# Tokens sorted by expert inside their tile, and moved to the experts' pages in runs of 64 rows

## The chip, the cores and the metric

One Trainium2 chip, one core of it. The metric is the device time of one launch in microseconds (us). The time before is the median of 14 runs, 3545.61 us (3536.86 to 3567.67).

The engines are called PE (matrix products; PEld is its load of weights), DVE (vector), ACT (scalar), POOL (GpSimd) and SP (sync). Each takes its instructions in program order from a queue of its own, and the transfers (DMAs) that an engine issues stand in that queue between its other instructions.

## The reference

A graph layer, and behind it a layer of experts, on x with 12500 rows (tokens) of 256 numbers and 212500 edges that are sorted by dst:

```
msgs = layernorm(x)[src] * edge_weight[:, None]
x = x + segment_sum(msgs, dst) @ W.T + b

h = layernorm(x)
probs = softmax(h @ gate_w + gate_b)               # 8 experts
idx, prb = argmax(probs), the probability there
pos = how many earlier tokens chose the same expert
kept = pos < C                                     # C = 1954
y = relu(h @ w1[idx] + b1[idx]) @ w2[idx] + b2[idx]   # 256 -> 1024 -> 256
x = x + nan_to_num(y * (prb * kept))
```

All numbers are float32. The tokens of an expert have places 0, 1, 2, ... in the order of their row, and those at C and above get nothing from the expert.

## The kernel before

**Units.** An *edge tile* is 128 edges; there are 1661 (`KT`). A *node tile* is 128 tokens; there are 98, each the target of some 17 edge tiles. Node tiles go in *chunks*: eleven of 8, then 5, 4 and 1. A *page* is 128 rows of one expert in the tensor `buf` in DRAM, 16 pages an expert and two spare. A row of `buf` has 260 numbers (`RW`): the token after the graph layer, its mean and inverse deviation, its probability, and its row number. A row of a page with number `FILL` (1048576) is empty; an output scatter drops rows out of bounds.

**Phases.** `table()` writes the normalized x to DRAM (`feat`); the first 112 edge tiles are gathered meanwhile from x itself. Then the loop `while alive or pages or b or outs` (L822) does the rest. One turn of it issues, in this order:

1. `gather(s)` (L582, POOL): an indirect transfer of 128 rows of 1 KB from `feat` to one of 32 buffers `m`.
2. one item of `pool_q`, if there is one: a `put` (L341, POOL), an indirect transfer that scatters the rows of one node tile (`rt`) to their pages by the index `to`. If there is none, one step of `outs`, the end of a page's work: DVE makes `z` and `tok` (L522), and `send` (L525, POOL) scatters the page's rows to the output.
3. one-hots (L590, DVE, four at a time, 8 ahead of the products) and `product(done)` (L599, PE), the edge product of the tile gathered 16 turns (`LEAD`) earlier; 15 products sum up to one group (`ws`, L602, ACT).
4. one step of `nodes()`, one of `fill()` or `check()` at the beginning, and one of `experts()`.

`nodes()` goes over the chunks. For each node tile it loads x (`xt`, L623, three tiles ahead, issued by ACT), places the groups' sums by products with shifted one-hots (L635), copies (L639), multiplies by W (L644) and adds (L647). At the end of the chunk `route` stores the chunk's rows to the output (`store_rows`, L170, issued by ACT), normalizes, gates (L274, L279), and finds each token's place: `pp` counts the tokens of each expert before a token in its tile (`pp[:, 0]`) and in the whole tile (`pp[:, 1]`), `run` counts over the tiles (L321 and the line after it). The puts of the chunk then wait in `pool_q`. `listing` (L370 is in it, on DVE) finds which pages have become full. When `pool_q` is empty, these pages are queued:

```
SLOTS = [(2, n) for n in (0, 3, 4, 4, 4, 4, 4, 4, 4, 2)] + [(1, n) for n in (10, 4, 3)]
```

(pages at a time, and how many times, after each chunk but the last: chunk 0 none, chunk 1 three pairs, and so on). After the last chunk come the 8 partly filled pages, whose places `last` gives.

`experts()` takes queued pages. `load` (SP) reads the page's row and expert into registers (L432, L435), then issues the page's transfer (`pg`, L439) and `weights` its biases (L446, L448) and weights (L450, L452), whose addresses are in those registers. `LOADED - 3` = 17 turns later `fresh` (L459, DVE) normalizes the page, at 20 turns `turn` (L468) transposes it, then `products` (L483, L487, L494) is spread over turns, 3.0 turns a step for a pair (`PACE`). `fill()` writes empty rows to all of `buf` at the start of the loop, 13 transfers of SP.

**Order.** Everything runs under `tc.manual_schedule()`: each engine does its instructions in the order in which the program issues them. Waits come from the data (and from buffers that come free); `declare_no_dep` takes back those between puts and between puts and page loads.

After the loop, `rest()` runs only if more full pages are left, and a second path (`tc.If(some > 0)`) only if `n_bad`, a count of edges that lie out of the expected windows, isn't 0.

Of the kernel before, what the change touches and what calls it, by code (L numbers as in the profile page):

```python
# [18 lines left out]
P = 128  # L19
# [26 lines left out]
FILL = float(1 << 20)  # L46


SLOTS = [(2, n) for n in (0, 3, 4, 4, 4, 4, 4, 4, 4, 2)] + [(1, n) for n in (10, 4, 3)]
# [9 lines left out]
LOADED = 20  # L59
PACE = {1: 2.3, 2: 3.0}  # L60


# [32 lines left out]
def gnn_moe_kernel(ctx: ExitStack, tc: tile.TileContext, x, src, dst, ew, wT, gb, gate_w, gate_b,  # L95
# [53 lines left out]
    nc.vector.tensor_scalar(need, even, float(P), float(P), op0=ALU.mult, op1=ALU.add)  # L149
    n_bad = consts.tile([1, 1], I32, name="n_bad")  # L150

    gb_sb = consts.tile([P, D], F32, name="gb_sb")
# [4 lines left out]
    keep = ctx.enter_context(tc.tile_pool(name="keep", bufs=1))  # L157
    run = keep.tile([P, E], F32, name="run")
    posted = keep.tile([P, 1], F32, name="posted")
    place_of = keep.tile([P, 1], F32, name="place_of")  # L160
# [58 lines left out]
    class Ffn:  # L219
        def __init__(self, p3, p4, ps_m, ps_t, ps_h, ps_y):  # L220
            self.p3, self.p4 = p3, p4
            self.ps_m, self.ps_t, self.ps_h, self.ps_y = ps_m, ps_t, ps_h, ps_y
            self.puts, self.sends, self.loads = [], [], []
            self.paired = False
# [6 lines left out]
            nc.vector.memset(taken, 0.0)  # L231

        def fill(self):
# [11 lines left out]

        def route(self, rt, ln, t0, nt, rows):
            p3 = self.p3
            yield
            r = yield from ln_scale(p3, ln, nt, rows)
            o = store_rows(out, rt[:, :, :D], t0, nt, rows, nc.scalar)  # L250
            for i in self.sends:
# [99 lines left out]

            self.put = [(put, j) for j in range(nt)]


# [57 lines left out]
        def last(self):  # L412
            p3 = self.p3
            c8 = p3.tile([P, E], F32, name="c8")
            nc.vector.tensor_mul(c8, run, mine)
            c = p3.tile([P, 1], F32, name="c1")
            nc.vector.tensor_reduce(c, c8, axis=AX.X, op=ALU.add)
            nc.vector.tensor_scalar(c, c, float(C), page0, op0=ALU.min, op1=ALU.subtract)
            some = p3.tile([P, 1], F32, name="some")
            nc.vector.tensor_scalar(some, c, 1.0, None, op0=ALU.is_ge)  # L420
            nc.vector.scalar_tensor_tensor(some, c, float(P), some, op0=ALU.is_lt, op1=ALU.mult)
            nc.vector.tensor_scalar(c8, mine, some, None, op0=ALU.mult)
            pi = self.psum("pi")
            nc.tensor.matmul(pi[0:1, :E], page_of[:, 0:1], c8, start=True, stop=True)
            lp = p3.tile([1, E], I32, name="lp", bufs=1)
            nc.vector.tensor_scalar(lp, pi[0:1, :E], float(NP_ * P), None, op0=ALU.add)
            return lp

        def load(self, of, li, i, e=None):
            p4 = self.p4  # L430
            at = li[0:1, 0, i:i + 1] if e is None else li[0:1, e:e + 1]
            row = nc.values_load(at, engines=[mybir.EngineType.SP], min_val=0, max_val=NP_ * P,  # L432
                                 skip_runtime_bounds_check_because="a page, or the empty one")
# [4 lines left out]
            pg = p4.tile([P, 2, RW], F32, name="pg", bufs=4)  # L438
            self.loads.append(nc.sync.dma_start(  # L439
                pg[:, :of, :], buf[ds(row, of * P), :].rearrange("(a p) d -> p a d", p=P)))  # L440
# [118 lines left out]
    with tc.tile_pool(name="edges", bufs=1) as edges:  # L559
# [8 lines left out]
        with tc.tile_pool(name="p2", bufs=32) as p2, tc.tile_pool(name="p2h", bufs=12) as p2h, \  # L568
# [8 lines left out]
            sums, ms, hs = {}, {}, {}  # L577
            pool_q, pages = [], []

# [25 lines left out]
            def nodes():  # L605
# [10 lines left out]
                for c, (t0, nt, rows) in enumerate(CHUNKS):  # L616
                    rt = p3.tile([P, CH, RW], F32, name="rt")
                    ln = ln_new(p3)
                    for t in range(t0, t0 + nt):
                        for i in range(len(xs), min(t + 3, NT)):  # L620
                            x_ = p3.tile([P, D], F32, name="xt", bufs=4)
                            r = min(P, N - i * P)
                            nc.scalar.dma_start(x_[:r, :], x[i * P:i * P + r, :])  # L623
                            xs.append(x_)
# [24 lines left out]
                        ln_stats(ln, x1, t - t0, rows)  # L649
                    yield from ffn.route(rt, ln, t0, nt, rows)  # L650
                    pool_q.extend(ffn.put)
                    last = c == len(CHUNKS) - 1
                    if last or SLOTS[c][1]:
# [4 lines left out]
                        while pool_q:  # L658
                            yield
# [62 lines left out]
            def check():  # L722
# [17 lines left out]
                nc.tensor.matmul(pc, ones[:, 0:1], cnt, start=True, stop=True)  # L740
                nc.vector.tensor_scalar(n_bad, pc, -1.0, float(P * KT), op0=ALU.mult, op1=ALU.add)

# [79 lines left out]
            while alive or pages or b or outs:  # L822
                s = now[0]
                if s < KT:
                    gather(s)
                if pool_q:
                    f, j = pool_q.pop(0)
                    f(j)
                else:
                    for o in outs[:1]:  # L830
                        if next(o, None) is None:
                            outs.remove(o)
                if made < min(KT, max(done, s - LEAD) + AHEAD):
# [14 lines left out]
                now[0] += 1  # L848
            for f, j in pool_q:
                f(j)  # L850
            ffn.rest()

    some = nc.values_load(n_bad[0:1, 0:1], min_val=0, max_val=P * KT,
                          skip_runtime_bounds_check_because="a count of edges")
    with tc.If(some > 0):
# [132 lines left out]
```

## Time and profile before

| | |
|---|---|
| median of 14 runs | 3545.61 us |
| profiled execution | 3540.53 us |
| its span | 3538.7 us |
| mean granted PE clock | 0.765 |
| bytes moved | 455.60 MB, mean 129 GB/s |

The **span** is from the first to the last instruction of one profiled execution; all durations below are from it. In the list of engines, the first number is busy time, then its share of the span and the number of instructions. A **group** line has line, engine, operation, output<-inputs and count; then the busy us and the mean ns of one; then the idle us of that engine just before these instructions, and what ended most of it ("issue" is: nothing that the profile shows). A line in the queue of SP or POOL (`SPq`, `POOLq`) is the issuing of a transfer; the name before it is of the instruction. The granted clock is the share of full speed that PE was given.

In the page's 40 slices of 88.5 us each, the busy tenths and the clock are:

```profile
PE   2356344663674656556475466466554646446777
...
DVE  5654122332332224223232233233322323223343
ACT  4520000110110101011011011011110101001233
POOL 5555665645644544553644555554555464555211
PEclk9768676886887878677686688687777778678889
DMA  7674334423522522532522442352252242254556
```

The last two to three slices are behind the last gather.

### The profile page before, as it was taken

The numbers are of one execution on the slowest core, as the hardware profiler recorded it, in microseconds if no ns is written. First come the engines' busy times: TensorE is split into PE (matmuls) and PEld (weight loads), VectorE is DVE, ScalarE is ACT, GpSimd is POOL, SyncE is SP. The second block draws the span as 40 slices with busy tenths as digits, with TensorE's granted clock in tenths as the row PEclk, the third lists the DMA queues.
The fourth block names the chain that finished last, engine by engine and source line by source line (L and its number), as shares of the span: only waits on it lengthen the run. The fifth ranks groups of instructions, "written<-read, shape, count | busy, mean of one in ns | idle before, by whom it ended". The sixth has DMA issues, their size and how long they took to land. (4 is left out here: it accounts for less than half of the span.)

```text
span 3538.7 us, 30236 instructions
## 1 busy us (share of the span) xinstructions
PE 2016.8 (57%) x9082; PEld 1683.2 (48%) x9082; DVE 1155.8 (33%) x4287; ACT 500.8 (14%) x1315; POOL 1785.8 (50%) x1859
## 2 busy tenths in 40 slices
PE   2356344663674656556475466466554646446777
PEld 1245243552563545445364355355444535345677
DVE  5654122332332224223232233233322323223343
ACT  4520000110110101011011011011110101001233
POOL 5555665645644544553644555554555464555211
PEclk9768676886887878677686688687777778678889
DMA  7674334423522522532522442352252242254556
GB/s 237 216 243 149 95 97 126 135 77 113 170 70 88 184 72 76 183 97 61 185 90 81 128 139 86 100 164 63 90 186 77 75 145 66 85 163 158 174 188 220
DMA packets 264700, 455.60 MB, mean 129 GB/s; under 512 B 44799, under 2 KB 190406, under 8 KB 264520
## 3 DMA queue, kind: packets, MB, share of 16 engines
q0 software_dynamic: 88800, 240.41, 22.0%
q1 hardware_dynamic: 136210, 174.68, 15.3%
q10 hardware_dynamic: 39510, 38.41, 3.3%
q8 instruction: 77, 1.26, 0.1%
q14 instruction: 103, 0.84, 0.1%
HBM read 387.86 MB, written 67.83 MB: 129 GB/s over the span
## 5 line engine op out<-in xcount | busy, mean ns | idle before, releaser
L582 POOL DMA_INDIRECT m<-feat,src_i x1549 | 1480.9, 956 | 683.5 <-issue 371.4
L599 PE MATMUL pw<-m,h 128*128 128x256 f32 x3322 | 995.0, 432 | 193.9 <-DVE h L590 119.1
L599 PEld LDWEIGHTS pw<-m,h 128*128 128x128 f32 x3322 | 700.5, 221 | 320.6 <-DVE h L590 128.4
L590 DVE TENSOR_SCALAR h<-cols,rel,w_sb 128x128 f32<-128x128 f32 x1549 | 454.2, 356 | 735.3 <-remote 384.0
L644 PE MATMUL ms<-wT_sb,aT 128*128 128x256 f32 x392 | 145.2, 507 | 561.4 <-ACT aT L639 424.8
L483 PE MATMUL ph<-gT,w_sb 128*128 128x256 f32 (+1 forms) x1856 | 364.3, 346 | 136.2 <-issue 116.1
L525 POOL DMA_INDIRECT out<-z,tok x91 | 92.4, 1015 | 643.7 <-DVE tok L522 471.5
L494 PE MATMUL py<-w_sb,hT 128*128 128x256 f32 x1456 | 381.5, 406 | 35.2 <-issue 34.8
L483 PEld LDWEIGHTS ph<-gT,w_sb 128*128 128x128 f32 x1856 | 307.1, 199 | 171.3 <-issue 118.1
L644 PEld LDWEIGHTS ms<-wT_sb,aT 128*128 128x128 f32 x392 | 90.6, 246 | 603.9 <-ACT aT L639 446.1
L635 PE MATMUL ms<-s,ws 128*128 128x128 f32 x1116 | 191.6, 310 | 290.5 <-issue 156.1
L647 DVE TENSOR_TENSOR rt<-xt,ms 128x256 f32<-128x256 f32 x98 | 41.1, 419 | 910.4 <-PE ms L644 566.3
L635 PEld LDWEIGHTS ms<-s,ws 128*128 128x128 f32 x1116 | 185.0, 221 | 311.3 <-issue 162.9
L494 PEld LDWEIGHTS py<-w_sb,hT 128*128 128x128 f32 x1456 | 293.8, 207 | 80.9 <-issue 38.9
L341 POOL DMA_INDIRECT buf<-rt,to x98 | 103.4, 1056 | 330.5 <-DVE c L370 242.7
L487 ACT ACTIVATE hT<-ph,b_sb 128x256 f32<-128x256 f32 (+1 forms) x464 | 167.0, 426 | 616.0 <-remote 241.1
L279 PE MATMUL ms<-gw_sb,xT 128*128 128x8 f32 x392 | 70.2, 288 | 169.8 <-ACT xT L274 103.0
L279 PEld LDWEIGHTS ms<-gw_sb,xT 128*128 128x128 f32 x392 | 67.1, 239 | 205.8 <-ACT xT L274 136.7
L639 ACT COPY aT<-ms 128x256 f32<-128x256 f32 x98 | 36.5, 372 | 803.6 <-remote 638.4
L582 POOL DMA_INDIRECT m<-in_x,src_i x112 | 107.9, 964 | 81.3 <-ACT junk L767 33.3
L602 ACT COPY ws<-pw 128x256 f32<-128x256 f32 x111 | 41.2, 371 | 694.5 <-remote 335.4
L281 DVE TENSOR_TENSOR lgs<-ms,gateb_sb 128x8 f32<-128x8 f32 x98 | 16.2, 165 | 290.5 <-PE ms L279 154.4
(159 smaller groups left out, 1217.2 us busy)
## 6 DMA issues: line engine op xcount, KB each, us to landing
w_sb<-in_w SPq DMA_DIRECT2D x116, 1024.0 KB
m<-feat,src_i POOLq DMA_INDIRECT x1549
buf<-fill SPq DMA_DIRECT2D x13, 1300.0 KB
xt<-in_x ACTq DMA_DIRECT2D x97, 128.0 KB
xt<-in_x SPq DMA_DIRECT2D x12, 1024.0 KB
feat<-xn ACTq DMA_DIRECT2D x12, 1024.0 KB
out<-rt ACTq DMA_DIRECT2D x11, 1024.0 KB
pg<-buf SPq DMA_DIRECT2D x33, 260.0 KB
```

The lines of the kernel that those rows point to most:

```text
L279: nc.tensor.matmul(pl[:rows, :], xT[:, k, :rows], gw_sb[:, k, :], start=(k == 0), stop=(k == 1))
L341: s = nc.gpsimd.indirect_dma_start(out=buf[:, :], out_offset=bass.IndirectOffsetOnAxis(ap=to[:, j, :], axis=0), in_=rt[:rows, j, :], in_of ...
L483: nc.tensor.matmul(ph[:, c:c + n], w1_sb[:, k, f * P:(f + 1) * P], xT[:, k * n:(k + 1) * n], start=(k == 0), stop=(k == 1))
L487: nc.scalar.activation(hT[:, f, :n], ph[:, c:c + n], AF.Relu, bias=b1_sb[:, f:f + 1])
L494: nc.tensor.matmul(py[:, a, :], hT[:, f, a * P:(a + 1) * P], w2_sb[:, f, :], start=(f == 0), stop=(f == F // P - 1))
L525: s = nc.gpsimd.indirect_dma_start(out=out[:, :], out_offset=bass.IndirectOffsetOnAxis(ap=to[:, a, :], axis=0), in_=z[:, a, :], in_offset= ...
L582: nc.gpsimd.indirect_dma_start(out=m, out_offset=None, in_=x[:, :] if k < RAW else feat[:, :], in_offset=bass.IndirectOffsetOnAxis(ap=src_ ...
L590: nc.vector.tensor_scalar(h, cols, rel[:, k:k + 1], w_sb[:, k:k + 1] if w is None else w, op0=ALU.is_equal, op1=ALU.mult)
L599: nc.tensor.matmul(product.pw, hs.pop(k), ms.pop(k), start=(j == 0), stop=last)
L602: nc.scalar.copy(ws, product.pw)
L635: nc.tensor.matmul(pa[:, k * P:(k + 1) * P], sums[g][:, k * P:(k + 1) * P], shifts[t, g], start=(g == gs[0]), stop=(g == gs[-1]))
L644: nc.tensor.matmul(px[:rows, :], aT[:, k * P:k * P + rows], wT_sb[:, k, :], start=(k == 0), stop=(k == 1))
```

## The change

**The sort.** After the gate, `pos` is now a token's place in its own tile, by expert and within the expert by row: `off` is the sum of the tile's counts of the experts before, and `pre = pp[:, 0] + off`. `sort` makes for each tile a 128x128 one-hot `perm` of `pos` (DVE), multiplies it with the tile's rows of `rt` (PE, 128x260), and copies the product back to `rt` (ACT). The chunk's sorted rows go by one transfer of SP to a tensor in DRAM, `by_expert[c % 3]`, which has 64 empty rows behind the chunk's 1024.

**The moves.** In place of 8 puts a chunk has 64 moves (8 tiles, 8 experts). A move copies 64 rows (`RUN`), from the tile's first token of that expert in `by_expert` to the place in `buf` where the expert's next token belongs; both rows are read into SP's registers from the tile `runs`, 9 register loads for the 8 moves of a tile (`READS`). What a move copies beyond the expert's tokens is written over by the expert's next move, and a move waits for the move before it of the same expert. Four moves are issued a turn (`MOVES`), and a step of `outs` now comes in every turn, also while moves are left. As before, the chunk's pages are queued when no move is left.

**What follows from it.** The rows behind the last token of a partly filled page now hold other tokens, so `last` makes `none`, which adds `SKIP` to their number in `fresh`. A tile with more than 64 tokens of one expert is counted in `most` and sets `n_bad`. The loads of `xt` and the store of the chunk's rows to the output are issued by SP instead of ACT. `fill` also fills the ends of the three `by_expert`. The second path still scatters.

```diff
+RUN = 64
...
+MOVES = 4
+READS = [((0, 0, 2), (1, 0, 2)), ((0, 2, 2),), ((1, 2, 2),), ((0, 4, 2),), ((1, 4, 2),), ((0, 6, 2),),
+         ((1, 6, 1),), ((1, 7, 1),)]
...
+    by_expert = [dram.tile([CH * P + RUN, RW], F32, name=f"by_expert{i}") for i in range(3)]
...
         def fill(self):
...
+            for s in by_expert:
+                nc.sync.dma_start(s[CH * P:, :], fill[:RUN, :])
...
-        def route(self, rt, ln, t0, nt, rows):
+        def route(self, rt, ln, t0, nt, rows, place=None):
...
-            o = store_rows(out, rt[:, :, :D], t0, nt, rows, nc.scalar)
+            o = store_rows(out, rt[:, :, :D], t0, nt, rows, nc.sync)
...
+            if place is not None:
+                runs = p3.tile([P, CH, 2, E], I32, name="runs")
+                off = p3.tile([P, CH, E], F32, name="off")
+                nc.vector.memset(off[:, :, 0:1], 0.0)
+                for e in range(E - 1):
+                    nc.vector.tensor_add(off[:, :nt, e + 1], off[:, :nt, e], pp[:, 1, :nt, e])
+                nc.vector.tensor_add(pre, pp[:rows, 0, :nt, :], off[:rows, :nt, :])
+                nc.vector.tensor_add(runs[0:1, :nt, 0, :], off[0:1, :nt, :],
+                                     tokc[0:1, :nt, None].to_broadcast([1, nt, E]))
+                much = p3.tile([1, 1], F32, name="much")
+                nc.vector.tensor_reduce(much, pp[0:1, 1, :nt, :], axis=AX.XY, op=ALU.max)
+                nc.vector.tensor_tensor(most, most, much, op=ALU.max)
             for j in range(nt):
-                nc.vector.tensor_add(pre[:, j, :], pp[:rows, 0, j, :], run[:rows, :])
+                if place is None:
+                    nc.vector.tensor_add(pre[:, j, :], pp[:rows, 0, j, :], run[:rows, :])
+                else:
+                    nc.vector.scalar_tensor_tensor(runs[0:1, j, 1, :], run[0:1, :], float(C), pages_of,
+                                                   op0=ALU.min, op1=ALU.add)
                 nc.vector.tensor_add(run, run, pp[:, 1, j, :])
...
+            if place is not None:
+                nc.vector.tensor_scalar_add(pos, pos, -1.0)
+                yield from self.sort(rt, pos, runs, place, nt, rows)
+                return
...
+        def sort(self, rt, pos, runs, place, nt, rows):
+            for j in range(nt):
+                r = self.p3.tile([P, P], F32, name="perm")
+                nc.vector.tensor_scalar(r[:rows, :], cols[:rows, :], pos[:, j, :], None,
+                                        op0=ALU.is_equal)
+                yield
+                ps = self.psum("ps")[:, :RW]
+                nc.tensor.matmul(ps, r[:rows, :], rt[:rows, j, :], start=True, stop=True)
+                nc.scalar.copy(rt[:, j, :], ps)
+            yield
+            nc.sync.dma_start(place[:nt * P, :].rearrange("(j p) d -> p j d", p=P), rt[:, :nt, :])
+            at = {}
+
+            def move(j, e):
+                for i, f, n in READS[e]:
+                    _, v = nc.values_load_multi_w_load_instructions(
+                        runs[0:1, j, i, f:f + n], engines=[mybir.EngineType.SP], min_val=0,
+                        max_val=((E - 1) * PE_ * P + C if i else CH * P),
+                        skip_runtime_bounds_check_because="rows of the chunk, and of the pages")
+                    at.update(((i, f + a), v[a]) for a in range(n))
+                s = nc.sync.dma_start(buf[ds(at[1, e], RUN), :], place[ds(at[0, e], RUN), :])
+                for i in self.moves:
+                    if i is not self.moved[e]:
+                        tc.declare_no_dep(s.ins, i.ins, reason="another expert's, or one before that")
+                for i in self.loads:
+                    tc.declare_no_dep(s.ins, i.ins, reason="pages that are read are full")
+                self.moves.append(s)
+                self.moved[e] = s
+
+            self.put = [(move, j, e) for j in range(nt) for e in range(E)]
...
         def last(self):
...
+            cs = p3.tile([P, E], F32, name="cs", bufs=1)
+            nc.vector.tensor_scalar(cs, c8, c, None, op0=ALU.mult)
+            pc = self.psum("pc")[:, :E]
+            nc.tensor.matmul(pc, ones, cs, start=True, stop=True)
+            self.none = p3.tile([P, E], F32, name="none", bufs=1)
+            nc.vector.tensor_scalar(self.none, pc, pcol, float(SKIP), op0=ALU.is_le, op1=ALU.mult)
...
         def fresh(self, of, pg):
             xg = self.p4.tile([P, 2, D], F32, name="xg")
+            if self.part[id(pg)] is not None:
+                nc.vector.tensor_add(pg[:, 0, D + 3:RW], pg[:, 0, D + 3:RW], self.part[id(pg)])
...
-                            nc.scalar.dma_start(x_[:r, :], x[i * P:i * P + r, :])
+                            nc.sync.dma_start(x_[:r, :], x[i * P:i * P + r, :])
...
-                if pool_q:
-                    f, j = pool_q.pop(0)
-                    f(j)
-                else:
-                    for o in outs[:1]:
-                        if next(o, None) is None:
-                            outs.remove(o)
+                for f, j, e in moves[:MOVES]:
+                    f(j, e)
+                del moves[:MOVES]
+                for o in outs[:1]:
+                    if next(o, None) is None:
+                        outs.remove(o)
```

More of the change, by code (lines that the diff above doesn't have):

```diff
@@ L158, in gnn_moe_kernel @@
     run = keep.tile([P, E], F32, name="run")
+    most = keep.tile([1, 1], F32, name="most")
     posted = keep.tile([P, 1], F32, name="posted")
@@ L231, in __init__ @@
             nc.vector.memset(taken, 0.0)
+            nc.vector.memset(most, 0.0)
+            self.moved, self.moves = [None] * E, []
         def fill(self):
@@ L577, in gnn_moe_kernel @@
             sums, ms, hs = {}, {}, {}
-            pool_q, pages = [], []
+            moves, pages = [], []
             def gather(k):
@@ L649, in nodes @@
                         ln_stats(ln, x1, t - t0, rows)
-                    yield from ffn.route(rt, ln, t0, nt, rows)
-                    pool_q.extend(ffn.put)
+                    yield from ffn.route(rt, ln, t0, nt, rows, by_expert[c % 3])
+                    moves.extend(ffn.put)
                     last = c == len(CHUNKS) - 1
+                    if last:
+                        nc.vector.scalar_tensor_tensor(n_bad, most, float(RUN), bad, op0=ALU.is_gt,
+                                                       op1=ALU.add)
                     if last or SLOTS[c][1]:
@@ L657, in nodes @@
                         li = ffn.li
-                        while pool_q:
+                        while moves:
                             yield
@@ L848, in gnn_moe_kernel @@
                 now[0] += 1
-            for f, j in pool_q:
-                f(j)
             ffn.rest()
-    some = nc.values_load(n_bad[0:1, 0:1], min_val=0, max_val=P * KT,
-                          skip_runtime_bounds_check_because="a count of edges")
+    some = nc.values_load(n_bad[0:1, 0:1], min_val=0, max_val=P * KT + 1,
+                          skip_runtime_bounds_check_because="a count of edges, and one")
     with tc.If(some > 0):
```

8 lines of the change are left out of this document (7 added, 1 removed).

## The prediction

> **What bounds the kernel now.** I read the page's groups first, then stretches of one chunk, then the queue of SP. The profiled execution took 3540.5 us, 3538.7 of them its span; the median of the 14 runs, 3545.6, is 0.14% above it.
>
> ```profile
> PE 2016.8 (57%) x9082; PEld 1683.2 (48%) x9082; DVE 1155.8 (33%) x4287; ACT 500.8 (14%) x1315; POOL 1785.8 (50%) x1859
> ...
> L582 POOL DMA_INDIRECT m<-feat,src_i x1549 | 1480.9, 956 | 683.5 <-issue 371.4
> ...
> L525 POOL DMA_INDIRECT out<-z,tok x91 | 92.4, 1015 | 643.7 <-DVE tok L522 471.5
> ...
> L341 POOL DMA_INDIRECT buf<-rt,to x98 | 103.4, 1056 | 330.5 <-DVE c L370 242.7
> ```
>
> No engine is full. POOL issues 1549 gathers, and the scatters stand between them in the same queue. A scatter into the pages (L341) waits for the vector engine to reach its place in the program, on average 3.4 us, in truth about 30 us once a chunk (the longest is 31.1); an output scatter (L525) waits the same way, four times a chunk. What that does is seen in one chunk, cut at those waits (from the page scatter at 1112.2 to the next at 1393.4; columns: us, then busy us and count of PE, PEld, DVE, ACT, POOL, then clock, DMA share, GB/s):
>
> ```profile
> 1112.20:1163.60 51.40, 17.70 (x69) 14.19 (x70) 12.16 (x46) 1.12 (x3) 39.45 (x40) 0.63 0.51 161
> 1163.60:1220.40 56.80, 43.87 (x191) 37.34 (x190) 19.67 (x64) 6.96 (x17) 26.71 (x29) 0.86 0.54 173
> 1220.40:1277.90 57.50, 32.67 (x154) 28.15 (x153) 15.41 (x50) 6.12 (x15) 27.74 (x30) 0.76 0.31 95
> 1277.90:1332.00 54.10, 33.45 (x153) 28.48 (x152) 16.53 (x54) 6.80 (x16) 27.64 (x29) 0.81 0.25 76
> 1332.00:1393.40 61.40, 35.13 (x166) 28.89 (x165) 19.43 (x89) 10.17 (x22) 23.99 (x26) 0.78 0.23 71
> ```
>
> The chunk takes 281.2 us for about 136 turns of the loop at L822 (one gather and one edge product each). Inside one of these stretches:
>
> ```profile
> 1220.40:1235.80 15.40, 15.23 (x78) 13.05 (x76) 6.53 (x24) 3.73 (x9) 11.74 (x13) 1.00 0.59 192
> 1235.80:1260.10 24.30, 0.03 (x1) 0.00 (x0) 0.00 (x0) 0.04 (x1) 15.04 (x16) 0.54 0.31 92
> 1260.10:1277.90 17.80, 17.41 (x76) 15.10 (x77) 8.88 (x26) 2.36 (x6) 0.95 (x2) 0.86 0.05 15
> ```
>
> For 15 us POOL and the others work side by side; then POOL goes on with a gather each 1.25 us while PE, DVE and ACT all but stop for 24 us; POOL then stands at the next output scatter, and the others catch up. I call the middle part a **quiet stretch**. The trace shows it after some 10 to 25 us of unbroken gathers, every time, and it ends about 4 us after they end; it doesn't show why. SP is slowed in it as well:
>
> ```profile
> 1137.15 0.70 SPq L446 DMA_DIRECT2D b_sb<-in_b  x1
> 1142.82 0.71 SPq L448 DMA_DIRECT2D b_sb<-in_b  x1
> 1147.76 0.69 SPq L450 DMA_DIRECT2D w_sb<-in_w  x1
> 1153.35 0.69 SPq L452 DMA_DIRECT2D w_sb<-in_w  x1
> ...
> 1215.29 0.34 SPq L448 DMA_DIRECT2D b_sb<-in_b  x1
> 1215.87 0.38 SPq L450 DMA_DIRECT2D w_sb<-in_w  x1
> 1216.48 0.38 SPq L452 DMA_DIRECT2D w_sb<-in_w  x1
> ```
>
> Outside a quiet stretch two transfers whose address is in a register follow each other in 0.6 us, inside one in 5.4 us. This pair of numbers carries the prediction.
>
> **Part 1: the 98 scatters and their wait go.** POOL spends 8 x (1.06 + 0.30) = 11 us a chunk on them and 30 us waiting. But the wait is the others' catching up, and without it POOL runs on until the products that free its 32 buffers hold it (16 turns ahead), so most of it returns at the next output scatter. So I compare stretches. The last one (61.4 us, cut short by the page scatter) becomes an ordinary one, 57.5: -4. The first two (108.2 us, 57 turns) lose the 11 us of scatters and, by the order of the changed program, three turns at 1.8: -16. Sum **-20 us a chunk**. Bounds: 0 (the wait only moves) and -41 (all of it was lost time).
>
> **Part 2: the sort.** Per tile one product of the kind of the edge product with 260 columns for 256: 995.0 us / 1661 = 0.60 us, so 4.8 us a chunk of 8. DVE makes a 128x128 comparison per tile (nearest row s<-cols,win, L612, 298 ns): 2.4 us; and some 9 more small ones a chunk than now (the row L321, 165 ns): 1.5. ACT copies 98 tiles (row L602, 371 ns: 36 us) and no longer issues 98 x loads (L623, median 334 ns) and 14 stores (401 ns): 38 us; that cancels. PE and DVE hold the catching up, so I charge it in full: **+9 us a chunk**; bounds 0 (it falls into quiet stretches) and +11 (products at the 0.86 us of the halved clock).
>
> For the transfers taken from ACT, the rule of the Trainium skill (DMA: Bandwidth & Descriptors, section Issuing engines are not separate DMA queues) is that the engine that starts a transfer matters only for its own issue time. By it ACT gains no more than those 38 us, which I already set against the copies.
>
> **Part 3: 784 moves in the queue of SP.** That is the largest term. A move is a register load (L432 today), the address arithmetic and the transfer:
>
> ```profile
> L432 SPq TENSOR_LOAD <-li x50: 3/278/1387, 570.7 to 3432.5; - x50
> ```
>
> 0.33 us from one load to the next instruction plus the 0.6 above: 0.93 us undisturbed. A chunk has 64 moves: 60 us, with 8 more loads 62. Behind them in the same queue stand the chunk's first page (L439) and its weights, and now also the next x tiles. The program gives them 34 turns: the moves are let go four a turn, then LOADED - 3 = 17 turns pass until DVE takes the page (L459).
>
> How long are 34 turns? Before the first output scatter some 11 turns at 1.2 us, POOL standing: 13 us, of which 8 go to the sorted tile's store, as its 1 MB sister out<-rt took 6.5 and has to land; 5 are left. Then 23 turns. In the trace the 22 products from the first page scatter to L459 take 59 us in four of the chunks and up to 65 in the others; less 10 us of scatters, 49 us. About half of these are quiet (in the chunk above 1123.4 to 1127.9 and 1136.2 to 1160.4, 29 of 59), so 24 quiet and 25 not. SP gets through (5 + 25) / 0.93 = 32 moves, and 24 / 5.4 = 4 more. **28 are left**: DVE waits for 28 x 0.93 = 26 us and 2 us for the page. In order, behind it: the one-hots, then the products, then POOL's buffers. **+28 us a chunk.** Bounds: 0 if SP keeps up, and 64 x 5.4 - 54 = +290 if the moves keep the stretch quiet themselves. I take the mixed value, since the rows of the same place in the program are mixed.
>
> Another rule of the Trainium skill speaks against the change: DMA: Bandwidth & Descriptors, section Latency and other measured facts, puts the floor of a register load at about 600 ns. The trace's median is 278. By the page's figure 72 loads would add 23 us a chunk to the 28; the trace decides.
>
> The moves' bytes (784 x 66.6 KB = 52 MB, for 13 MB scattered) go beside a DMA share of 0.23 to 0.54; I charge nothing. If that cover were missing, gathers would land late, with 16 turns (20 us) of lead before anybody notices.
>
> **Part 4: x tiles behind the fill.** At the start SP's queue writes 13 x 1300 KB into the pages (issued from 215.1 to 271.8 us, the DMA share of 200 to 300 us is 0.79). The x loads now stand between them: the fourth behind five fills, the sixth behind all. In the trace the sixth tile is added at 241.1; the fills are done near 283. Some of the 42 us is made up: **+30 us once**, bounds 0 and +42.
>
> **Sum.** Ten chunks have 64 moves and pages behind them (chunk 0 has no pages, the last three are short and end when other pages keep PE busy): 10 x (-20 + 9 + 28) + 30 = +200. 3540.5 + 200 = **3740 us**, 5.5% above the median.
>
> **Rivals.**
> - **SP keeps up** (faster). Without page scatters the gathers are held by the products more often, quiet stretches shrink, and 54 us of undisturbed SP take 58 moves: nothing of note is left over. It decides from the point where the quiet share of those turns falls below a tenth. For it: in 1163.6 to 1220.4, where gathers wait for products, PE is busy 43.9 of 56.8 us. Against it: between 410.4 and 560 us, with no output scatter at all, gathers still come in runs of 15 to 25 and PE has gaps. Then 3540 + 10 x (-20 + 9) + 30 = 3460; with the full -41, 3250.
> - **Even.** The page is late by the 11 us that the other parts bring: 3540 to 3570.
> - **SP becomes the bound.** Moves during gathers stay slow; with half of them at 5.4, 64 x 3.2 = 203 us, 149 too many: 3540 + 10 x 138 + 30 = 4950.
> - **The change does not do what it says**: a tile with more than 64 tokens of one expert sets n_bad, and the second path runs. Counted from the inputs, the largest is 46; no chance.
>
> **Chances.** Forecast (3570 to 3960) 0.50; SP keeps up 0.35, of it 0.07 under 3400; even 0.07; SP the bound 0.08. Range 3400 to 3960, which leaves 0.15 out. By sign, 0.2% being about what a measurement of this kernel tells from no change: faster 0.36, same 0.04, slower 0.60.
>
> **What would show it.** Right: DVE idle at the page's first use (now L459) until the page's transfer, 20 to 40 us a chunk; SP issuing moves 0.9 us apart outside quiet stretches and some 5 us inside; POOL's waits moved from the page scatter to gathers held by products and to the output scatter. Wrong: no wait at L459 and chunks of 265 us (part 3 falls), or moves slow with POOL standing, or x tiles awaited in every chunk.

## The result

The changed kernel takes **4123.31 us** (median of 10, 4109.06 to 4133.39) for 3547.47: **1.162** times the time before, interval 1.160 to 1.164. The forecast was slower, 3740 us, at most 3960. The sign was right, and that the vector engine waits behind the moves; how long it waits, and for which transfer, was not.

The runs are not all of the same chip, and the kernel before is not equally fast on all of them: 3499 to 3549 us on some (called *long* here), 2569 to 2572 us on one (*short*), which shows no quiet stretches. So every run is compared with the kernel before on its own chip. Which chip the first two profiles come from is not on record; both show the times and the quiet stretches of a long one.

From the page of the changed kernel (profiled execution 4119.81 us, span 4118.0), the engines and the groups that answer to those shown of before:

```profile
PE 2077.3 (50%) x9280; PEld 1725.3 (42%) x9280; DVE 1198.4 (29%) x4524; ACT 534.6 (13%) x1413; POOL 1679.0 (41%) x1761
...
L668 POOL DMA_INDIRECT m<-feat,src_i x1549 | 1477.6, 954 | 1437.9 <-PE pw L685 856.6
...
L733 DVE TENSOR_TENSOR rt<-xt,ms 128x256 f32<-128x256 f32 x98 | 41.1, 419 | 1580.7 <-DMA xt<-in_x 777.5
L611 POOL DMA_INDIRECT out<-z,tok x91 | 92.8, 1019 | 903.5 <-DVE tok L608 541.8
```

In the page of before, the line that answers to L733 waits for products, and no transfer is named:

```profile
L647 DVE TENSOR_TENSOR rt<-xt,ms 128x256 f32<-128x256 f32 x98 | 41.1, 419 | 910.4 <-PE ms L644 566.3
```

PE has 60 us more of work (it has the 196 products of the sort besides) in 580 us more of span. POOL now waits twice as long for gather buffers (1437.9 us for 683.5), which PE frees, and DVE has a wait that it did not have: 777.5 us at L733, the addition of the x tile, for the transfer of that tile. Of these, 745 are one wait of 71 to 79 us in each of ten chunks. One of them in the queue of SP (us, duration, line, transfer):

```profile
1560.86 0.39 SPq L407 DMA_DIRECT2D by_expert<-rt  x1
1565.55 118.18 SPq L418 DMA_DIRECT2D buf<-by_expert  x64
1685.34 0.41 SPq L523 DMA_DIRECT2D pg<-buf  x1
1685.96 0.36 SPq L530 DMA_DIRECT2D b_sb<-in_b  x1
1686.51 0.35 SPq L532 DMA_DIRECT2D b_sb<-in_b  x1
1687.10 0.38 SPq L534 DMA_DIRECT2D w_sb<-in_w  x1
1687.72 0.38 SPq L536 DMA_DIRECT2D w_sb<-in_w  x1
1688.15 0.75 SPq L709 DMA_DIRECT2D xt<-in_x  x1
```

The sorted chunk is stored, then 64 moves take 118 us, then come the page and its 2 MB of weights, and only then the x tile. The same time in stretches, cut at the store, the first move, the beginning and end of a quiet stretch, DVE's stop, the last move, and the x tile's landing (columns as in the prediction's stretches):

```profile
1560.90:1565.60 4.70, 4.70 (x25) 4.20 (x24) 1.71 (x9) 0.00 (x0) 0.00 (x0) 1.00 0.66 227
1565.60:1580.00 14.40, 14.07 (x77) 12.17 (x76) 9.62 (x33) 1.65 (x4) 4.06 (x4) 1.00 0.24 74
1580.00:1616.00 36.00, 7.27 (x25) 5.55 (x23) 2.58 (x10) 0.37 (x1) 23.64 (x25) 0.62 0.37 108
1616.00:1622.60 6.60, 3.57 (x12) 3.22 (x13) 4.02 (x15) 0.74 (x2) 3.87 (x5) 0.56 0.34 97
1622.60:1683.20 60.60, 3.72 (x15) 2.88 (x13) 0.05 (x1) 0.00 (x0) 7.50 (x8) 0.56 0.23 66
1683.20:1698.80 15.60, 0.00 (x0) 0.00 (x0) 0.00 (x0) 0.00 (x0) 0.00 (x0) 0.50 0.80 239
1698.80:1898.90 200.10, 130.96 (x595) 110.43 (x596) 69.16 (x254) 31.28 (x74) 97.74 (x102) 0.82 0.35 110
```

For 76 us (the fifth and sixth line) hardly anything works but SP and its transfers: PE 3.7 us, DVE 0.05, POOL 7.5. The chunk of 136 turns takes 336.7 us for 283.4 (gather 436 to gather 1524, eight chunks). What a move is made of shows in the rows of its two lines:

```profile
L413 SPq TENSOR_LOAD <-runs x882: 2/472/2732, 363.5 to 3996.7; - x177
```

```profile
L418 SPq MOVE buf<-by_expert x1568: 2/29/1530, 367.2 to 3997.1; - x196
L418 SPq FUSED_REGOPS  x784: 2/55/1395, 367.1 to 3997.0; - x196
L418 SPq DMA_DIRECT2D buf<-by_expert x784: 1/521/1845, 368.4 to 3997.2; - x196
```

A load of 0.472 us, the address in 0.055, two register moves of 0.029, the transfer's issue of 0.521, and 0.2 between them: **1.31 us** (the median from one move to the next). In a quiet stretch SP takes about 0.7 us for each of these instructions and another 0.7 between them, 7.1 us for a move; a stretch inside one, and one outside, of the same length:

```profile
1594.00 14.99 SPq L418 DMA_DIRECT2D buf<-by_expert  x3
```

```profile
1631.09 15.06 SPq L418 DMA_DIRECT2D buf<-by_expert  x12
```

### The profile page after: what moved, and what is told of

It is laid out like the page before. It is cut to its first block, busy times and chain, and to the rows that moved or that the text cites. A ratio compares the mean times of both kernels' runs of the same rounds, so it can differ in the third digit from the quotient of the medians.

```text
span 4118.0 us, 34817 instructions
## 1 busy us (share of the span) xinstructions
PE 2077.3 (50%) x9280; PEld 1725.3 (42%) x9280; DVE 1198.4 (29%) x4524; ACT 534.6 (13%) x1413; POOL 1679.0 (41%) x1761
## 5 line engine op out<-in xcount | busy, mean ns | idle before, releaser
L668 POOL DMA_INDIRECT m<-feat,src_i x1549 | 1477.6, 954 | 1437.9 <-PE pw L685 856.6
L733 DVE TENSOR_TENSOR rt<-xt,ms 128x256 f32<-128x256 f32 x98 | 41.1, 419 | 1580.7 <-DMA xt<-in_x 777.5
L554 PE MATMUL pT<-ident,xg 128*128 128x128 f32 x182 | 42.5, 359 | 768.0 <-DVE xg L545 748.6
L580 PE MATMUL py<-w_sb,hT 128*128 128x256 f32 x1456 | 393.1, 416 | 48.5 <-issue 47.3
L554 PEld LDWEIGHTS pT<-ident,xg 128*128 128x128 f32 x182 | 29.0, 182 | 780.5 <-DVE xg L545 717.0
L580 PEld LDWEIGHTS py<-w_sb,hT 128*128 128x128 f32 x1456 | 302.9, 213 | 114.1 <-issue 70.5
L404 PE MATMUL ms<-rt,perm 128*128 128x260 f32 x196 | 80.9, 504 | 201.8 <-DVE perm L400 190.9
L557 ACT COPY gT<-pT 128x512 f32<-128x512 f32 (+1 forms) x58 | 28.9, 498 | 1167.0 <-PE pT L554 801.9
L404 PEld LDWEIGHTS ms<-rt,perm 128*128 128x128 f32 x196 | 45.4, 247 | 220.2 <-DVE perm L400 183.4
```

The lines of the kernel that those rows point to most:

```text
L404: nc.tensor.matmul(ps, r[:rows, :], rt[:rows, j, :], start=True, stop=True)
L554: nc.tensor.transpose(pt[:, k * n + a * P:k * n + (a + 1) * P], xg[:, a, k * P:(k + 1) * P], ident)
L580: nc.tensor.matmul(py[:, a, :], hT[:, f, a * P:(a + 1) * P], w2_sb[:, f, :], start=(f == 0), stop=(f == F // P - 1))
L668: nc.gpsimd.indirect_dma_start(out=m, out_offset=None, in_=x[:, :] if k < RAW else feat[:, :], in_offset=bass.IndirectOffsetOnAxis(ap=src_ ...
```

## The experiments

**Theory A** (the prediction's, with other sizes): SP works off 64 moves as one block, and what stands behind them is late, whatever it is. **B**: only the x tiles are late. **C**: the bytes of the moves are the price. **Q**: the quiet stretches are. In the table, "chunk" is a chunk of 136 turns as above, "behind" the time from the last gather to the end; intervals in brackets.

| run | chip | us | ratio to before | chunk | behind |
|---|---|---|---|---|---|
| before (prediction) | long | 3540 | 1 | 283.4 | 206 |
| after (result) | long | 4123 | 1.162 [1.160, 1.164] | 336.7 | 281 |
| before_again | long | 3500 | 1.000 [0.997, 1.003] | 278.9 | 207 |
| after_again | long | 4078 | 1.165 [1.160, 1.170] | 332.8 | 281 |
| third_after | short | 3071 | 1.194 [1.191, 1.197] | 234.8 | 286 |
| x_act | short | 2994 | 1.166 [1.162, 1.169] | 227.7 | 284 |
| before_x_sp | short | 2583 | 1.006 [1.003, 1.008] | 194.2 | 191 |
| fixed | short | 2640 | 1.027 [1.024, 1.030] | 196.8 | 243 |
| later40 | short | 2628 | 1.024 [1.020, 1.029] | 188.9 | 333 |
| moves1 | long | 3692 | 1.056 [1.051, 1.060] | 287.0 | 394 |
| hybrid | long | 3502 | 1.002 [1.000, 1.005] | 275.3 | 315 |
| best10 | long | 3490 | 0.983 [0.979, 0.987] | 275.6 | 216 |
| best10m2 | long | 3781 | 1.064 [1.060, 1.069] | 312.6 | 208 |
| before_sort | long | 3603 | 1.015 [1.011, 1.019] | 290.7 | 209 |
| before_b20 | long | 3015 | 0.849 [0.846, 0.853] | 229.5 | 208 |
| after_b20 | short | 3105 | 1.209 [1.206, 1.211] | 235.4 | 288 |
| after_b20_2 | short | 3102 | 1.204 [1.201, 1.208] | 235.3 | 287 |
| best10_b20 | short | 2538 | 0.989 [0.985, 0.992] | 186.5 | 200 |
| best10_b20_2 | short | 2535 | 0.985 [0.983, 0.988] | 186.8 | 199 |
| best10_b17 | short | 2582 | 1.005 [1.003, 1.007] | 186.4 | 197 |

The expectations of x_act, fixed, before_x_sp and later40 are in us of a long chip, but these ran on the short one; they are compared as ratios to 3547 us (3950 to 4080 us is 1.11 to 1.15).

**x_act**: what SP took over from ACT is given back.

```diff
-                            nc.sync.dma_start(x_[:r, :], x[i * P:i * P + r, :])
+                            nc.scalar.dma_start(x_[:r, :], x[i * P:i * P + r, :])
...
-            o = store_rows(out, rt[:, :, :D], t0, nt, rows, nc.sync)
+            o = store_rows(out, rt[:, :, :D], t0, nt, rows, nc.scalar)
```

> The x tiles and the chunk's rows to the output are issued by ACT again; the rest is the changed kernel. Theory A (SP's queue as a whole is late: 64 moves take 113 us of it, and the x tile is only the first thing behind them that somebody needs): the wait of 72 to 78 us a chunk at the x tile goes, and DVE waits 50 to 65 us a chunk at the page (fresh) instead; 3950 to 4080 us. Theory B (only the x tiles are late, the pages come in time): no such wait at the page, 3400 to 3550. Theory C (the moves' bytes, read and written beside the gathers, are the price): 4080 to 4130, little changed.

The wait moved. Of x_act's page, DVE's idle time before the x tile has no transfer any more, and before the page it has:

```profile
L545 DVE TENSOR_SCALAR xg<-pg 128x256 f32<-128x256 f32 x91 | 35.2, 416 | 760.9 <-DMA pg<-buf 760.9
...
L733 DVE TENSOR_TENSOR rt<-xt,ms 128x256 f32<-128x256 f32 x98 | 41.1, 419 | 277.9 <-PE ms L730 273.9
```

57 to 64 us in each of ten chunks, 60.2 on average, as A had it; the ratio came out above A's. B falls: the x tiles were only the first to be missed. The moves of one chunk, now on the short chip, with the same 64 in one block:

```profile
1141.64 85.79 SPq L418 DMA_DIRECT2D buf<-by_expert  x64
```

**fixed**: as many moves of the same size without registers. They go to fixed places, so the output is not the reference's; and each move also waits for the one before it.

```diff
-                for i, f, n in READS[e]:
-                    _, v = nc.values_load_multi_w_load_instructions(
...
-                s = nc.sync.dma_start(buf[ds(at[1, e], RUN), :], place[ds(at[0, e], RUN), :])
+                s = nc.sync.dma_start(buf[e * PE_ * P + chunk * P + j * 16:, :][:RUN, :],
+                                      place[j * P + e * 16:, :][:RUN, :])
                 for i in self.moves:
-                    if i is not self.moved[e]:
+                    if i is not self.moved[e] and i is not self.moves[-1]:
```

> The same 64 moves a chunk of the same size, but from and to fixed addresses, so that no register is loaded and no address worked out; the output is not the reference's, as the pages hold tokens of other experts. The x tiles stay on SP. A: a move costs SP 0.4 to 0.6 us outside the quiet stretches and 0.7 to 1.4 inside, 64 of them 30 to 50 us a chunk; the wait at the x tile falls below 15 us a chunk; 3430 to 3560 us. B says the same, as the x tile comes early. C: the bytes are the same, so over 4000.

```profile
1049.76 41.15 SPq L412 DMA_DIRECT2D buf<-by_expert  x64
```

With the same bytes the ratio is 1.027 where the changed kernel on that chip has 1.194, so C falls. A move takes 0.65 us here, 64 of them 41, for 1.34 and 85 with registers (third_after, below). A's number was missed all the same: DVE still waits 36 us a chunk, since on this chip it is at the x tile 30 us after the store, when 26 moves are left (16 us), and behind them the page and its weights take 6 us to issue and the x tile 14 to land.

**before_x_sp**: the transfers of ACT put on SP, alone.

```diff
-                            nc.scalar.dma_start(x_[:r, :], x[i * P:i * P + r, :])
+                            nc.sync.dma_start(x_[:r, :], x[i * P:i * P + r, :])
```

(and the same for the chunk's rows to the output.)

> The kernel before, with only the x tiles and the chunk's rows to the output issued by SP instead of ACT. A: without moves in SP's queue the x tiles are in time, but for the fill at the start: 3540 to 3575 us, no wait of DVE at the x tile over 15 us after 350 us. Rival: SP's queue already stands at the page loads (for buffers that come free late) and the x tiles are late without any move: over 3600.

13 us (2582.55 - 2569.97), as expected, and no wait at the x tile behind the start is over 13 us. SP's queue is no bad place for these transfers as long as no block of moves stands in it.

**later40**: x_act, and the first page of a chunk is used 40 turns later.

```diff
-                        ready.append([now[0], ffn.load(*pages.pop(0)), None, None])
+                        what = pages.pop(0)
+                        wait = LATER if len(what) == 3 and what[2] == 0 else 0
+                        ready.append([now[0] + wait, ffn.load(*what), None, None])
```

> As x_act, and the first page of each chunk is used 40 turns later, so that the queue of SP has 74 turns (some 140 us) for the 64 moves and the page. A: the moves take SP as long as in the changed kernel, but neither the x tile nor the page is awaited for more than 10 us; what is left is the gain of the puts less the sort, 3430 to 3520 us. B: as x_act. C: over 4000.

Half right. The chunk falls from 227.7 to 188.9 us, below the 194.2 of before_x_sp, but 13 to 34 us of wait are left: the 74 turns lasted 72 to 84 us, not the 140 that I had taken from the trace of before, as turns without page products are short. And 142 us are lost behind the last gather, where the pages that were put off are done.

**before_again** and **after_again**, both kernels unchanged:

> The kernel before, unchanged. In the runs of the last four kernels it took 2570 us where the profile of the prediction has 3540: it was run again for a profile beside theirs. If the quiet stretches are what the two differ by: about 2570 us, PE busy over 90% in unbroken gather runs also after 20 us, a turn of some 1.4 us, and the wait of an output scatter (L525) hardly costs. If they are there at 2570 too, the difference is elsewhere (DMA, clock).

> The changed kernel, unchanged, beside the four kernels before. Theory A (SP's queue is late by its block of 64 moves at 1.31 us): 64 moves in 84 to 90 us a chunk, DVE waits 60 to 80 us a chunk at the x tile, 1.16 to 1.25 of the kernel before, no faster than x_act (1.166). Theory Q (it is the quiet stretches that make the moves slow, and the kernel slower): without quiet stretches under 1.08.

**third_after**, the changed one again:

> The changed kernel, unchanged, once more. Where the kernel before takes 2570: 84 to 90 us for 64 moves, 70 to 80 us of waiting a chunk at the x tile, 1.17 to 1.21 (A); under 1.08 (Q). Where it takes 3500: 1.16 as before.

before_again and after_again ran on a long chip, so they repeat the first two profiles and neither explain the short one nor test Q: in after_again the moves of a chunk take 110 us, not the expected 84 to 90, and DVE waits 70 to 79. third_after, on the short chip, is the test of Q, and Q falls: without quiet stretches the moves take 84.6 us (1.34 each), DVE waits 72 to 79 us a chunk, and the ratio is no smaller.

```profile
L733 DVE TENSOR_TENSOR rt<-xt,ms 128x256 f32<-128x256 f32 x98 | 41.1, 419 | 1061.5 <-DMA xt<-in_x 841.1
```

**moves1**: `MOVES = 1` instead of 4, nothing else.

> The changed kernel with one move let go in a turn instead of four (MOVES = 1), all else the same. A: the x tiles and weights now stand between the moves instead of behind a block of 64, and the page comes 17 turns after the last move; SP is behind the others by 64 x 1.31 - 64 x 1.1 = 13 us at the end of a chunk's moves; DVE waits under 20 us a chunk at the x tile and under 10 at the page; 0.99 to 1.05 of the kernel before, where the changed one has 1.16. Theory C (the bytes of the moves, or SP's time as a whole, are the price): above 1.12, as the moves are as many and as large.

One constant takes 46 us from a chunk (332.8 to 287.0). Weights and x tiles now stand between moves; DVE still waits 353 us for x tiles, in 22 waits, 25 to 41 us a chunk where under 20 was expected, and the ratio, 1.056, is just above the 0.99 to 1.05 of A. Of the 192 us that it is slower than the kernel before, 188 are added behind the last gather. That the pages come 48 turns later, and the last ones have no gathers to hide behind, is the guess that hybrid and best10 test.

**hybrid**: moves1 and x_act, and the last three chunks are placed by scatters. **best10**: the last four (`c < 10`).

```diff
-                    yield from ffn.route(rt, ln, t0, nt, rows, by_expert[c % 3])
+                    yield from ffn.route(rt, ln, t0, nt, rows, by_expert[c % 3] if c < 11 else None)
```

> One move a turn, x tiles and the chunk's rows to the output issued by ACT, and the last three chunks (5, 4 and 1 node tiles) placed by scatters as before. A: no wait at x tile or page over 10 us a chunk; the chunks get 5 to 10 us shorter than before, and the time behind the last gather, which was 190 us with scatters and 284 to 332 with moves in the last four kernels, is back under 210; 0.96 to 1.00 of the kernel before. C: above 1.08.

> As hybrid (one move a turn, x tiles and output rows by ACT), but the last four chunks are placed by scatters instead of the last three. hybrid was 114 us ahead of the kernel before at the last gather and gave 109 back behind it. Theory T: it gave them back because the 10 single pages that follow chunk 10 came 64 turns later; with scatters there the time behind the last gather is 210 to 260 us where before has 206, and the ratio to the kernel before is 0.965 to 0.985. Rival: the pages left over are those of the earlier chunks too, each a little late: still over 0.995.

hybrid has three waits of over 10 us at the page left before the last gather (37, 19 and 12), and one of 32 at it. It is 114 us ahead of before_again at its last gather (3181.7 for 3296.1) and gives 109 back behind it, 315 us where under 210 was expected; its chunk is 3.6 us shorter, not 5 to 10. best10 has 216 us behind the last gather, so theory T holds: the ten single pages after chunk 10 were late. Its waits at the page are 132 us in 16 times, 36 and 17 of them in the first two chunks. best10 is 1.7% faster than the kernel before, the first that beats it.

**best10m2**: best10 with `MOVES = 2`.

> best10 with two moves a turn. Theory A: SP falls behind by 64 x 1.31 us less 32 turns of 1.2 to 2.1, some 20 to 45 us, of which 17 turns of lead cover 20 to 30: DVE waits 0 to 20 us a chunk at the page, the pages come 32 turns earlier, 0.96 to 1.00. Rival (any block of moves is awaited in full): 40 us a chunk at the page, 1.05 or more.

The rival's number: DVE waits 35 to 54 us a chunk at the page, with 23 to 37 moves left when it stops, and the chunk is 37 us longer than best10's. So a lead of 17 turns behind 32 turns of moves does not cover what SP is behind; one move a turn does, nearly.

**before_sort**: the three steps of the sort added to the kernel before, to a tile that nobody reads.

> The kernel before with the sort's three steps added for each tile (one-hot on DVE, product of 260 columns on PE, copy by ACT to a spare tile that nobody reads); scatters stay. The prediction charged 7.5 us a chunk for these: 1.02 to 1.035 of the kernel before where nothing hides them, 1.00 to 1.01 if they fall into waits.

53.6 us (3602.84 - 3549.28) for 98 tiles: 4.4 us for a chunk of 8, where the prediction has 7.5. The chunks between gathers 436 and 1524, though, are longer by 7.3 (290.7 for the 283.4 of the first profile, whose chip is not on record). So the price is 4 to 7 us, and the ratio, 1.015, lies between the two ranges that were expected.

**before_b20**: `p2` with 20 buffers instead of 32.

> The kernel before with 20 buffers m instead of 32, so that POOL may run at most 4 gathers further ahead of the products than the order of the program has it. If the quiet stretches need a long run of gathers (over 15 us unbroken), there are fewer where they were, and the ratio is under 0.97; if they come whatever the run, or if gathers now land late, 0.99 to 1.05. On a chip without quiet stretches 0.99 to 1.01.

0.849, the largest gain of the study, and it has nothing to do with the change. Stretches of over 3 us in which PE, DVE and ACT all stand still sum to 308 us between the first 112 gathers and the last one; in the profile of before it is 936. POOL's own runs of over 15 us without a pause are 41 with 1037 us in all, for 56 with 1941. The slices of PE and POOL, of before_b20:

```profile
PE   2455556576678587588587587677677666567887
...
POOL 5566666666666666666666666666667666565211
```

**after_b20** (run twice), **best10_b20** (twice), **best10_b17**: the changed kernel and best10 with 20 buffers, and best10 with 17.

> The changed kernel with 20 buffers m instead of 32. Theory A (the block of 64 moves in SP's queue is the price, with or without quiet stretches): 64 moves in 84 to 105 us, DVE still waits 55 to 75 us a chunk at the x tile, 0.97 to 1.03 of the kernel before, which is 1.14 to 1.21 of the kernel before with 20 buffers (0.849). Theory Q (the quiet stretches make the loss): 0.84 to 0.92.

> The changed kernel with 20 buffers m, once more, for a place where the kernel before takes 3500. A: moves take 90 to 110 us a chunk, DVE waits 60 to 80 us at the x tile; 0.97 to 1.05 of the kernel before there. Q (the stretches make the loss): 0.84 to 0.92. If the kernel before takes 2570 again: 1.20 to 1.21 as the first time.

> best10 (one move a turn, x tiles and output rows by ACT, scatters in the last four chunks) with 20 buffers m. A: moves keep pace, and the gain of the puts less the sort (6 us a chunk at 32 buffers, less the tail) stays: 0.82 to 0.85 of the kernel before. Rival: with shorter turns (1.8 us for 2.05) SP's 1.31 us a move leaves less for weights, and the page is awaited again: 0.86 to 0.92.

> best10 with 20 buffers m, once more. Where the kernel before takes 3500: 0.80 to 0.85 of it, at or below the 0.849 of the kernel before with 20 buffers. Where it takes 2570: 0.985 to 0.992 as the first time.

> As best10_b20 with 17 buffers: POOL may be one gather ahead of the order of the program. If shorter runs of gathers mean fewer quiet stretches still: 0.76 to 0.82 of the kernel before. If the 20 buffers took all that can be had, or gathers now wait for products without need: 0.82 to 0.90.

All five ran on the short chip, where there are no quiet stretches to take away. So their ranges for a long chip are not tested; those that were given for the short one, 1.20 to 1.21 and 0.985 to 0.992, were met. after_b20 keeps its block of moves (84.6 us) and its wait (75 us a chunk). best10_b20 beats the kernel before by 1.1 to 1.5%, with a chunk of 186.5 us; 17 buffers lose that again in the first 300 gathers (gather 300 at 477 us for 439); the chunk is the same. What best10 with 20 buffers does on a long chip was not run.

## Why the prediction was wrong

**The step that failed** is in part 3: "0.33 us from one load to the next instruction plus the 0.6 above: 0.93 us undisturbed", and behind it "28 x 0.93 = 26 us and 2 us for the page". That DVE waits once a chunk, behind the moves, was right. Term by term, with the mean of the ten waits:

| | forecast | measured |
|---|---|---|
| from the store to DVE's stop, us | 62 | 55.8 |
| first move behind the store, us | 8 | 5.0 |
| moves issued by then | 36 | 20.7 |
| moves left | 28 | 43.3 |
| time for these, us | 26 | 59.6 |
| page, weights, x tile: issue and landing, us | 2 | 4.9 + 10.0 |
| wait, us | 28 | 74.5 |

My own working with the measured durations (1.31 us a move and 7.2 in a quiet stretch) gives (5 + 25) / 1.31 + 24 / 7.2 = 26 moves, 38 left, 50 us, and 15 behind them: 65. So the measured prices bring the forecast from 28 to within 10 us of the wait. The split of the time was not far off: by the same two prices, an estimate, the 20.7 moves in the 51 us behind the first mean 22 us undisturbed and 29 quiet. The trace of before had loads of one value and transfers with one address in a register. A move loads two values at once and has two such addresses, and its issue from DRAM to DRAM takes 0.52 us where the weights' takes 0.38. I took the nearest rows for the thing itself, and set no upper bound outside the quiet stretches. What is awaited was also named wrongly: I charged the page, which comes first, but the x tile stands behind the page's weights, 15 us and not 2. The prediction itself has "x tiles awaited in every chunk" among its signs of being wrong.

Two readings behind the 62 us were wrong as well, and cost less. The time from the first page scatter to the first page is not 59 to 65 us in every chunk of before: in three of ten (those at 1393, 1674 and 2531 us) it is 25 to 27, and the mean is 51. And the packets of the 1 MB transfer out<-rt are through 4.0 to 4.7 us after its issue in the trace of before, where I took 6.5; the first move came 5.0 us behind the store and not 8.

The prices of loads are in the trace of third_after: the loads of two values take 0.47 us (median of each of the seven places), those of one 0.27 to 0.28. The Trainium skill (Runtime: NRT & Kernel Launch, section Instruction fetch mechanics) gives about 200 ns a register for loads into a sequencer's registers; the step from one value to two, 0.20 us, agrees, though the first value costs 0.27 to 0.28, and though the page speaks of loads from HBM, while these read an SBUF tile. The rule that I weighed in the prediction (DMA: Bandwidth & Descriptors, section Latency and other measured facts), a floor of about 600 ns, does not hold for either kind of load. By 200 ns a register, an estimate from that page, the 128 values of a chunk's moves would be 26 us; measured are 9 x 8 loads at 0.47 or 0.28, 31 us, and I had charged 24.

**Parts 1 and 2**, -11 us a chunk. best10_b20 against before_x_sp, both on the short chip, is -7.7, but the two also differ in the buffers (with 17 the chunk is the same as with 20; 32 was not run) and in the queue of the x tiles. hybrid against before_again on the long one is -3.6, with waits at the page still in it. The sort cost 4 to 7 us (7.5 forecast, without the small ones), so the scatters were worth less than the 20: some 8 to 15, an estimate from these differences. Right in sign, in the bounds.

**A wait is not its length.** A chunk of the changed kernel is 53 us longer, not 74.5 - 11 = 63; on the short chip 41, with a wait of 75.3. That gathers run on into their buffers during the wait, so that less is waited for afterwards, is argued, not shown.

**Part 4**, +30 us once for the x tiles behind the fill: 11 to 13 us (x_act against third_after at gather 300, 423.7 for 435.1; before_x_sp in all). Inside the bounds of 0 and 42; at gather 300 the changed kernel was even 3 us ahead.

**What was left out**: "the last three are short and end when other pages keep PE busy". Behind the last gather it is 281 us for 206, and scatters in the last four chunks bring it back to 216.

**The sum**: 579 us of span. 52 at gather 436 (one of the ten waits lies before it), 8 x 53.3 = 426 to gather 1524, 26 to the last gather, 75 behind it. Of the rivals, none was right: SP did not keep up, nor did it become the bound in the way described, since most moves ran undisturbed (median 1.31 us on both kinds of chip). The range ended at 3960 because its upper end was the forecast's own, while the price of a move, the one unknown, had no end of its own.

## What to carry over

A block of small transfers in one queue is paid by what stands behind it, so count the queue's time by all its instructions (each register value, each address, each issue), and against the time until the first thing behind it is needed. Spreading the block over the loop (one move a turn) took 46 of 54 us a chunk back, without making a move cheaper (1.50 us from one to the next in moves1). And look at the end: what hides in the loop has nothing to hide behind after the last gather.

## What the runs showed of the hardware

The kernel before takes 3499 to 3549 us on the long chips and 2569 to 2572 on the short one, with the same instructions. What differs is the quiet stretches: those in which PE, DVE and ACT all stand still for over 3 us sum to 936 us in the profile of before and 854 in before_again, but to 31 in before_x_sp on the short chip, and the kernel takes some 950 us less there. The granted clock differs too (0.87 for 0.77; in the quiet stretch that the prediction shows it is 0.54). The slices of PE and POOL of before_x_sp, on the short chip:

```profile
PE   2464888698699698698698699698698798798797
...
POOL 7647677777777777777777777777777777777111
```

Here POOL goes on for 2092 us, gathers and scatters, without a pause of over 0.5 us, and PE stays busy; on the long chips PE, DVE and ACT all but stop, mostly after 10 to 25 us of unbroken gathers, and SP's instructions take 0.7 us each. It is not every time, as the prediction has it: of the 43 runs of over 18 us in the profile of before (behind the start), 38 bring a stretch in which all three stand still within 7 to 23 us, four only after 29 to 37, one none. With 20 buffers instead of 32, with which POOL's runs are shorter, the kernel before takes 15% less on a long chip. So the runs show that the stretches depend on the chip, or on what else goes with it (two of the three chips whose numbers are on record have them, one does not), and on how far POOL runs ahead; by which mechanism stays open. Of the two numbers of buffers tried on such a chip, 32 was too many.
